# A fifth tile for du times B in a selective-scan network, taken from the pool behind the scan inputs

## The chip, the cores and the metric

The kernel runs on one core of a Trainium2 chip as one launch. The metric is the time of an execution on the device in microseconds; three runs of the kernel before have a median of 8846.92 us (8845.23 to 8850.76). One further execution was profiled. All data is float32.

## The reference

Four images of 64x64 tokens with 128 channels pass through four layers. Layer 0 is a block around a selective scan in four directions, then an MLP; layer 1 is a self-attention over all 4096 tokens; layer 2 is a chain of convolutions of 1x1 and 3x3; layer 3 is a neighbourhood attention with a 7x7 window, then an MLP. What matters here is the scan: `xs` are the activations of 256 channels in four orders (by rows, by columns, and both backwards), and every channel has 16 states.

```
def step(h, t):
    x_t, d_t, B_t, C_t = t
    h = jnp.exp(d_t[..., None] * A) * h + (d_t * x_t)[..., None] * B_t[:, :, None, :]
    return (h, jnp.einsum('bkdn,bkn->bkd', h, C_t))
...
h0 = jnp.zeros((Bn, K, DI, N), input.dtype)
_, ys_l = jax.lax.scan(step, h0, scan_in)
```

## The kernel before, in words

`scan_inputs` computes, for an image, delta, du = delta times x, B and C, and writes them to HBM. `selective_scan` reads them back in chunks of `LC` = 512 steps. For each image there are 4 directions, 8 chunks, 2 halves of the channels, 4 groups of states (`j`) and 2 pairs (`pp`): 512 rounds an image, 2048 in all. A round, called a unit in what follows, does this:

- GpSimd makes `dB` = du times B as one 128x1024 product (L500 and L501), into one of 4 tiles that are used in turn.
- ScalarE makes dA = exp(A times delta) in two halves of 128x512, in PSUM, where there are 3 tiles for it (L506, L507).
- VectorE runs two scans of 512 steps, which read dA and dB (L509).
- The product of the states with C goes to VectorE as two 128x512 operations (L514) or, in some units (`ON_POOL`: 5 of 16 in the first image, 7 of 16 later), to GpSimd as one 128x1024 operation (L522). Its tile is `hc`, from the class `Products`. A product on GpSimd is given out 2 units late (`BEHIND`).
- TensorE sums over the states with a matrix of ones and zeros (L555), and ScalarE copies the last state for the next chunk (L516, L518).

SyncE issues the loads of delta and du (4 tiles each) and of the rows of B and C (4 tiles each, L494).

Beside the scan of image 1, 2 or 3 the program holds `rest` of the image before it: the output of layer 0 with its MLP (`scan_output`), layers 1 and 2, and the attention of layer 3; the MLP of layer 3 is given out together with the `scan_output` of the next image. The `rest` of the last image follows its scan.

No order is written out by hand. A scheduler in the compiler puts the instructions of each engine in one fixed order, by priorities and by its own timing of the instructions, and adds the waits. The scan counts its priorities from `SCAN_FIRST` = 10,000,000. Each engine then runs its queue in order, and an instruction whose tile is still being read by others waits at the head of it.

Tile pools are taken from the core's memory like a stack. When the inputs of all images are made, their pools are given back; the pool `ss_more` is then opened in that place and stays open until the scans are over. `S.products.widen(more, 4)` lets the hc tiles use it: after 40 further tiles, 4 of 10 come from there. The pools of `rest` lie behind it.

The lines that the change and the prediction touch are L435, L438 to L451 (`Products`), L500 (the dB tile), L507, L509, L514, L522, and L1743 (`widen`). The edge memsets of layer 2, L985 and L987, are the only other instructions on GpSimd that repeat in each image while scans run.

Of the kernel before, what the change touches and what calls it, by code (L numbers as in the profile page):

```python
# [28 lines left out]
F32 = mybir.dt.float32  # L29
# [13 lines left out]
LC = 512  # L43
# [24 lines left out]
def mid(ap, n):  # L68

    return bc(ap.unsqueeze(1), [ap.shape[0], n, ap.shape[1]])  # L70
# [29 lines left out]
class Together:  # L100
# [3 lines left out]
    def __init__(self, tc, K):  # L104
        self.tc, self.K, self.done = tc, K, None
# [57 lines left out]
def loader(tc, pool, A, layer):  # L163
    def load(name, shape, src=None):
        t = pool.tile(shape, F32, name=f"w{layer}_{name}")
        tc.nc.sync.dma_start(t, A[f"L{layer}_conv_{name}"] if src is None else src)
        return t

    return load
# [240 lines left out]
def make_scan(ctx, tc, K, A):  # L410

    nc = tc.nc
    S = SimpleNamespace()
    big = ctx.enter_context(tc.tile_pool(name="ss_big", bufs=1))
    S.pool = ctx.enter_context(tc.tile_pool(name="ss", bufs=2))
    S.psum = ctx.enter_context(tc.tile_pool(name="ss_ps", bufs=1, space=PSUM))
    load = loader(tc, big, A, 0)
    S.A = load("A_log", [128, KD, NJS, NPR, 2])
    nc.scalar.activation(S.A, S.A, AF.Exp)
    nc.vector.tensor_scalar_mul(S.A, S.A, -1.0)  # L420
    ds4 = load("Ds", [128, ND, KD])
    total = big.tile([128, ND], F32, name="Dsum")
    nc.vector.tensor_reduce(total, ds4, AX.X, ALU.add)
    S.skip = big.tile([128, ND, 128], F32, name="skip_diag")
    for d in range(ND):
        nc.scalar.activation(S.skip[:, d, :], K.ident, AF.Copy, scale=total[:, d : d + 1])

    S.pick = big.tile([128, 32], F32, name="pick")
    nc.gpsimd.memset(S.pick, 1.0)
    for base, sign in ((0, 1), (3, -1)):  # L430
        nc.gpsimd.affine_select(
            S.pick, S.pick, [[-4 * sign, 32]], ALU.is_ge, 0.0, base=base, channel_multiplier=sign
        )
    S.unit = 0
    S.products = Products(S.pool)  # L435
    return S


class Products:

    def __init__(self, pool):
        self.pool, self.more, self.turn = pool, None, 0

    def widen(self, pool, bufs):
        self.more, self.bufs, self.turn = pool, bufs, -40

    def tile(self):
        self.turn += 1
        if self.more is not None and self.turn > 0 and self.turn % (6 + self.bufs) < self.bufs:
            return self.more.tile([128, 2, LC], F32, name="hc", bufs=self.bufs)  # L450
        return self.pool.tile([128, 2, LC], F32, name="hc", bufs=6)  # L451


def selective_scan(tc, K, S, D, img):
# [9 lines left out]
    pool, psum, products = S.pool, S.psum, S.products  # L464
    waiting = []

    def settle(unit):
        while waiting and waiting[0][0] <= unit:
            waiting.pop(0)[1]()

    for k in ORDER:
# [4 lines left out]
        for i in range(NCH):  # L476
            c = NCH - 1 - i if back else i
            for hf in range(2):
# [11 lines left out]
                for j in range(NJS):  # L490
# [6 lines left out]
                    hcs, made = [], []  # L497
                    for pp in range(2):
                        pr = 2 * hf + pp
                        dB = pool.tile([128, 2, LC], F32, name="dB", bufs=4)  # L500
                        nc.gpsimd.tensor_mul(dB, dus[pp], mid(bt, 2))  # L501
                        on_pool = S.unit % 16 in ON_POOL[img > 0]
                        S.unit += 1
                        hc = products.tile()
                        for g in range(2):
                            dA = psum.tile([128, LC], F32, name="dA", bufs=3)  # L506
                            nc.scalar.activation(dA, dts[pp][:, g, :], AF.Exp, scale=S.A[:, k, j, pr, g : g + 1])  # L507
                            hg = hc[:, g, :] if on_pool else dA
                            nc.vector.tensor_tensor_scan(  # L509
                                hg[:, order], dA[:, order], dB[:, g, order],  # L510
                                0.0 if i == 0 else state[:, j, pr, g : g + 1], ALU.mult, ALU.add,
                            )
                            if not on_pool:
                                mm = nc.vector.tensor_mul(hc[:, g, :], dA, ct)  # L514
                                if i < NCH - 1:
                                    nc.scalar.copy(state[:, j, pr, g : g + 1], dA[:, last : last + 1])  # L516
                        if on_pool and i < NCH - 1:
                            nc.scalar.copy(state[:, j, pr, :], hc[:, :, last])  # L518
                        if on_pool:

                            def product(hc=hc, ct=ct, made=made):
                                made.append(nc.gpsimd.tensor_mul(hc, hc, mid(ct, 2)))  # L522

                            waiting.append((S.unit + BEHIND, product))
                        else:
                            made.append(mm)
                        hcs.append(hc)
                        settle(S.unit)
# [1169 lines left out]
def network(tc, A, out):  # L1698
    nc = tc.nc
    with ExitStack() as ctx:  # L1700
        nc.scalar.preload_act_table_set("natural_log_exp_and_others")
        K = make_consts(ctx, tc)
        dram = ctx.enter_context(tc.tile_pool(name="scratch", bufs=1, space=DRAM))

        def scratch(name, shape):
            return dram.tile(shape, F32, name=f"{name}_dram")

        D = SimpleNamespace()
        D.bias = scratch("bias", [len(BIAS_KINDS), 128, HEADS * 512])
        D.biasT = [[scratch(f"biasT{k}_{i}", [128, HEADS, LC]) for i in range(4)] for k in range(3)]  # L1710
        D.conv_diag = scratch("conv_diag", [128, ND, 9, 128])
        D.w2_norms = scratch("w2_norms", [128, len(NORMS2), 4])
        D.w2_cv4, D.w2_bias = scratch("w2_cv4", [128, 128]), scratch("w2_bias", [1, 128])
        for name, shape in (("sz", [128, ND, LC]), ("xc", [128, ND, LC]), ("y", [128, ND, LC])):
            setattr(D, name, [[scratch(f"{name}{b}_{c}", shape) for c in range(NCH)] for b in range(B)])
        for name, shape in (("delta", [128, ND, LC]), ("du", [128, ND, LC]), ("bc", [NS, 2, LC])):
            made = [
                [[scratch(f"{name}{b}_{k}_{c}", shape) for c in range(NCH)] for k in range(KD)] for b in range(B)
            ]
            setattr(D, name, made)  # L1720
        D.y_first = [[[scratch(f"y_first{b}_{k}_{c}", [128, ND, LC]) for c in range(NCH)] for k in range(2)] for b in range(B)]
        D.y_cols = [scratch(f"y_cols{b}", [NCH, 128, NCH, ND, RC * RC]) for b in range(B)]
        for name in ("x4", "x5"):
            setattr(D, name, [scratch(f"{name}_{b}", [NT, C]) for b in range(B)])
        D.shift = [scratch(f"shift{b}", [NJ, 128]) for b in range(B)]

        with ExitStack() as scan_ctx:
            S = make_scan(scan_ctx, tc, K, A)
            make_conv_diagonals(tc, K, A, D.conv_diag)
            with priority(tc, K, SCAN_FIRST // 2):  # L1730
                with tc.tile_pool(name="mk_w2", bufs=1, side="right") as pool:
                    make_layer2(tc, K, A, D, pool)
            scan_inputs(tc, K, A, D, 0)
            before = None
            for img in range(B):
                with priority(tc, K, SCAN_FIRST):
                    selective_scan(tc, K, S, D, img)
                if img == 0:
                    make_bias(tc, K, A, D.biasT)
                    for later in range(1, B):  # L1740
                        scan_inputs(tc, K, A, D, later)
                    more = scan_ctx.enter_context(tc.tile_pool(name="ss_more", bufs=1))
                    S.products.widen(more, 4)  # L1743
                else:
                    rest(tc, K, A, D, img - 1, before)
                    before = img - 1, out[img - 1]
            rest(tc, K, A, D, B - 1, before, scan_ctx.close, out[B - 1])
        needed = ctx.enter_context(tc.tile_pool(name="needed", bufs=1)).tile([1, 1], mybir.dt.int32, name="needed")
        bound_exceeded(tc, K, needed)
        with tc.If(nc.values_load(needed) > 0):  # L1750
            everything_again(tc, K, A, D, out)
# [80 lines left out]
```

## Time and profile before

| | |
|---|---|
| median of three runs | 8846.92 us (8845.23 to 8850.76) |
| profiled execution | 8838.78 us, its span 8837.0 us |
| mean granted clock of TensorE | 0.860 |
| busy in the span: PE, DVE, ACT, POOL | 7047.0, 7137.4, 5686.9, 7046.7 us |
| dB products on GpSimd | 2048, mean 2375 ns |
| hc products on GpSimd | 832, mean 2376 ns |
| scans on VectorE | 4096 (four groups of L509, mean 1207 to 1272 ns) |
| last dB product ends | 7630 us after the start |

PE is TensorE's matmuls, DVE is VectorE, ACT is ScalarE, POOL is GpSimd and SP is SyncE. A row of a group gives the line, the engine, the operation, what it writes and reads with shapes, the count, then the busy time in us, the mean of one in ns, and the idle time of the engine just before these instructions with what ended most of it. A row of the waits gives the waiting engine with tile and line, what released it, and then the total in us, the number of times and the longest. "issue" stands where the profile shows no releaser. The stages of the program overlap, so shares over the whole span say little of one stage.

### The profile page before, as it was taken

The numbers are of one execution on the slowest core, as the hardware profiler recorded it, in microseconds if no ns is written. First come the engines' busy times: TensorE is split into PE (matmuls) and PEld (weight loads), VectorE is DVE, ScalarE is ACT, GpSimd is POOL, SyncE is SP. The second block draws the span as 40 slices with busy tenths as digits, with TensorE's granted clock in tenths as the row PEclk, the third lists the DMA queues.
The fourth block names the chain that finished last, engine by engine and source line by source line (L and its number), as shares of the span: only waits on it lengthen the run. The fifth ranks groups of instructions, "written<-read, shape, count | busy, mean of one in ns | idle before, by whom it ended". The sixth has DMA issues, their size and how long they took to land. (4 is left out here: it accounts for less than half of the span.)

```text
span 8837.0 us, 102218 instructions
## 1 busy us (share of the span) xinstructions
PE 7047.0 (80%) x30532; PEld 2635.0 (30%) x30532; DVE 7137.4 (81%) x8531; ACT 5686.9 (64%) x11661; POOL 7046.7 (80%) x3079
## 2 busy tenths in 40 slices
PE   6745858687788898786788988877789887788988
PEld 2211313132332222333322223333322223344333
DVE  4788978787999999998899999998899999513433
ACT  5646767676676676666766676667766666454366
POOL 6888998989899999997799999998899989500000
PEclk8756869697799998898899998888899998899989
DMA  5777777777554556665455556575455565320020
GB/s 185 244 232 247 241 251 240 260 242 262 189 170 165 170 170 219 191 211 190 160 168 173 174 174 227 194 224 176 156 171 174 176 217 192 108 70 5 1 82 12
DMA packets 855474, 1572.03 MB, mean 178 GB/s; under 512 B 218341, under 2 KB 336764, under 8 KB 851197
## 3 DMA queue, kind: packets, MB, share of 16 engines
q1 hardware_dynamic: 724605, 1389.21, 48.1%
q10 hardware_dynamic: 130304, 176.19, 5.6%
q8 instruction: 245, 4.01, 0.2%
q14 instruction: 320, 2.62, 0.1%
HBM read 1273.92 MB, written 280.18 MB: 176 GB/s over the span
## 5 line engine op out<-in xcount | busy, mean ns | idle before, releaser
L501 POOL TENSOR_TENSOR dB<-du,b_rows 128x1024 f32<-128x1024 f32 x2048 | 4805.9, 2375 | 477.2 <-issue 124.7
L507 ACT ACTIVATE dA<-dt,w_A_log 128x512 f32<-128x512 f32 x4096 | 2781.9, 690 | 510.8 <-DVE hc L509 246.7
L509 DVE TENSOR_TENSOR_SCAN dA<-dA,state,dB 128x512 f32<-128x512 f32 x2128 | 2631.5, 1272 | 275.6 <-POOL dB L501 131.8
L522 POOL TENSOR_TENSOR hc<-hc,c_rows 128x1024 f32<-128x1024 f32 x832 | 1976.6, 2376 | 47.0 <-ACT state L518 21.7
L509 DVE TENSOR_TENSOR_SCAN hc<-dA,state,dB 128x512 f32<-128x512 f32 x1456 | 1801.1, 1267 | 180.5 <-ACT dA L507 105.8
L514 DVE TENSOR_TENSOR hc<-dA,c_rows 128x512 f32<-128x512 f32 x2432 | 1564.5, 675 | 74.4 <-PE py L555 59.3
L555 PE MATMUL py<-hc,pick 128*32 128x512 f32 x8192 | 1245.1, 683 | 392.0 <-POOL hc L522 299.8
L516 ACT COPY state<-dA 128x1 f32<-128x1 f32 x2128 | 326.9, 158 | 1271.7 <-DVE hc L514 1260.1
L845 PE MATMUL pa<-e,l_v 128*128 128x512 f32 x2048 | 1062.5, 651 | 20.3 <-ACT e L801 20.3
L797 PE MATMUL pair<-l_g,l_f 32*128 32x512 f32 x2048 | 532.8, 667 | 165.7 <-ACT e L801 119.1
L801 ACT ACTIVATE e<-pair 128x1024 f32<-128x1024 f32 (+1 forms) x448 | 508.4, 1135 | 231.4 <-PE pair L797 222.8
L985 POOL MEMSET l_h<- 64x128 f32 x8 | 1.6, 197 | 814.9 <-DVE l_h L959 814.9
L845 PEld LDWEIGHTS pa<-e,l_v 128*128 128x128 f32 x2048 | 374.3, 199 | 670.9 <-issue 615.1
L555 PEld LDWEIGHTS py<-hc,pick 128*32 128x32 f32 x8192 | 210.1, 116 | 1161.4 <-issue 471.1
L247 PE MATMUL ps<-band,w_conv_diag 128*128 128x504 f32 (+3 forms) x1152 | 500.4, 594 | 6.0 <-ACT delta L397 6.0
L1351 PE MATMUL pair<-table,ident 128*128 128x512 f32 x768 | 408.2, 657 | 98.7 <-ACT e L1361 76.2
L509 DVE TENSOR_TENSOR_SCAN dA<-dA,dB 128x512 f32<-128x512 f32 x304 | 356.1, 1212 | 66.3 <-POOL dB L501 52.5
L201 PE MATMUL ps<-ident,ln_xn 128*128 128x128 f32 x512 | 141.9, 371 | 325.2 <-ACT ln_xn L198 253.2
L328 POOL TENSOR_TENSOR du<-delta,xc 128x1024 f32<-128x1024 f32 x128 | 333.3, 2611 | 52.6 <-ACT delta L397 46.7
L1361 ACT ACTIVATE e<-pair 128x1024 f32<-128x1024 f32 (+1 forms) x224 | 254.8, 1137 | 178.6 <-PE pair L1355 177.8
L247 PEld LDWEIGHTS ps<-band,w_conv_diag 128*128 128x128 f32 x1152 | 221.3, 193 | 283.9 <-issue 263.8
L797 PEld LDWEIGHTS pair<-l_g,l_f 32*128 32x128 f32 x2048 | 140.6, 189 | 523.9 <-ACT e L801 264.4
(285 smaller groups left out, 8746.8 us busy)
## 6 DMA issues: line engine op xcount, KB each, us to landing
b_rows<-bc_dram SPq DMA_DIRECT2D x1024, 256.0 KB
c_rows<-bc_dram SPq DMA_DIRECT2D x1024, 256.0 KB
dt<-delta_dram SPq DMA_DIRECT2D x512, 512.0 KB
du<-du_dram SPq DMA_DIRECT2D x512, 512.0 KB
delta_dram<-delta ACTq DMA_DIRECT2D x128, 512.0 KB
du_dram<-du SPq DMA_DIRECT2D x128, 512.0 KB
table<-biasT_dram SPq DMA_DIRECT2D x72, 512.0 KB
y_first_dram<-y_sum ACTq DMA_DIRECT2D x128, 256.0 KB
```

The costliest lines, as they stand in the source:

```text
L247: mm = nc.tensor.matmul(out[:, r0 - row0 : r1 - row0, c0:c1], lhsT((dy + 1) * 3 + dx + 1), src[:, r0 + dy : r1 + dy, c0 + dx : c1 + dx], s ...
L328: nc.gpsimd.tensor_mul(du.rearrange("p d (a b) -> p d a b", b=H), deltas[b].rearrange("p d (a b) -> p d a b", b=H), tk,)
L501: nc.gpsimd.tensor_mul(dB, dus[pp], mid(bt, 2))
L507: nc.scalar.activation(dA, dts[pp][:, g, :], AF.Exp, scale=S.A[:, k, j, pr, g : g + 1])
L509: nc.vector.tensor_tensor_scan(hg[:, order], dA[:, order], dB[:, g, order], 0.0 if i == 0 else state[:, j, pr, g : g + 1], ALU.mult, ALU.add,)
L514: mm = nc.vector.tensor_mul(hc[:, g, :], dA, ct)
L522: made.append(nc.gpsimd.tensor_mul(hc, hc, mid(ct, 2)))
L555: mm = nc.tensor.matmul(py[0][32 * q : 32 * q + 32, :], S.pick, hcs[q // 2][:, q % 2, :], start=(k == 1 and j == 0), stop=(j == NJS - 1),)
L797: nc.tensor.matmul(ps[:, u, :], f[quad, t // 4, span(t % 4, 128)], g[quad, c, :], start=True, stop=True)
L801: made = nc.scalar.activation(e, ps, AF.Exp)
L845: nc.tensor.matmul(pa, v[:, 8 * q + t, :], es[q], start=(t == 0 and q == 0), stop=(t == 7 and q == 3),)
L1351: nc.tensor.matmul(ps[:, u, :], K.ident, t[:, u, :], start=True, stop=False)
```

## The change

The class `Products` becomes `Tiles`, which takes the name of the tile and the number in the first pool, so that it serves the dB tiles too. dB tiles come from it, 4 from the scan's own pool. When `ss_more` has been opened, `S.inputs.widen(more, 1)` gives it one more tile there: after 40 further tiles, every fifth dB tile comes from `ss_more`. The pool grows by 4 KB in each partition, and the pools of `rest` behind it begin 4 KB higher. The instructions are the same in number and kind.

```diff
     S.unit = 0
-    S.products = Products(S.pool)
+    S.products = Tiles(S.pool, "hc", 6)
+    S.inputs = Tiles(S.pool, "dB", 4)
     return S
-class Products:
-    def __init__(self, pool):
-        self.pool, self.more, self.turn = pool, None, 0
-    def widen(self, pool, bufs):
-        self.more, self.bufs, self.turn = pool, bufs, -40
+class Tiles:
+    def __init__(self, pool, name, bufs):
+        self.pool, self.name, self.bufs = pool, name, bufs
+        self.more, self.turn = None, 0
+    def widen(self, pool, extra):
+        self.more, self.extra, self.turn = pool, extra, -40
     def tile(self):
         self.turn += 1
-        if self.more is not None and self.turn > 0 and self.turn % (6 + self.bufs) < self.bufs:
-            return self.more.tile([128, 2, LC], F32, name="hc", bufs=self.bufs)
-        return self.pool.tile([128, 2, LC], F32, name="hc", bufs=6)
+        pool, bufs = self.pool, self.bufs
+        if self.more is not None and self.turn > 0 and self.turn % (self.bufs + self.extra) < self.extra:
+            pool, bufs = self.more, self.extra
+        return pool.tile([128, 2, LC], F32, name=self.name, bufs=bufs)
...
-                        dB = pool.tile([128, 2, LC], F32, name="dB", bufs=4)
+                        dB = S.inputs.tile()
                         nc.gpsimd.tensor_mul(dB, dus[pp], mid(bt, 2))
...
                     S.products.widen(more, 4)
+                    S.inputs.widen(more, 1)
```

## The prediction

> **What bounds the kernel now.** I read four views in this order: the page's busy times and groups, the busy times by stage, the waits of GpSimd (POOL) in one stage, and the timeline there. The page's chain that ended last covers only the final microseconds (it starts at about 8800 us) and says nothing on the scan. From the page, GpSimd and its two groups:
>
> ```profile
> PE 7047.0 (80%) x30532; PEld 2635.0 (30%) x30532; DVE 7137.4 (81%) x8531; ACT 5686.9 (64%) x11661; POOL 7046.7 (80%) x3079
> ...
> L501 POOL TENSOR_TENSOR dB<-du,b_rows 128x1024 f32<-128x1024 f32 x2048 | 4805.9, 2375 | 477.2 <-issue 124.7
> ...
> L522 POOL TENSOR_TENSOR hc<-hc,c_rows 128x1024 f32<-128x1024 f32 x832 | 1976.6, 2376 | 47.0 <-ACT state L518 21.7
> ```
>
> These two groups are nearly all of GpSimd's 7046.7 us, and the last dB ends at 7630 us: until there GpSimd is over 90% busy. One dB tile with its two scans (a "unit") costs it in images 1 to 3 2.375 + 7/16 x 2.376 = 3.41 us. Where its idle time lies is seen by stage; the columns are the stretch, its length, then busy time (and count) of PE, PEld, DVE, ACT and POOL, PE's clock, DMA share and GB/s:
>
> ```profile
> 2215.00:2580.00 365.00, 284.03 (x1264) 142.23 (x1260) 331.20 (x429) 240.82 (x542) 309.51 (x134) 0.83 0.56 180
> 2580.00:3250.00 670.00, 601.81 (x2444) 177.53 (x2442) 634.45 (x689) 453.11 (x861) 670.00 (x291) 0.92 0.52 172
> 3250.00:3400.00 150.00, 129.49 (x564) 39.99 (x561) 140.96 (x181) 104.96 (x227) 118.99 (x55) 0.87 0.55 174
> 3400.00:3980.00 580.00, 470.62 (x2678) 178.61 (x2677) 546.22 (x608) 375.48 (x772) 580.00 (x251) 0.88 0.65 209
> 3980.00:4445.00 465.00, 337.95 (x1364) 167.90 (x1364) 379.31 (x537) 324.23 (x735) 367.15 (x159) 0.82 0.54 174
> 4445.00:5150.00 705.00, 636.40 (x2618) 193.57 (x2610) 666.59 (x715) 474.14 (x904) 700.25 (x303) 0.94 0.53 172
> 5150.00:5310.00 160.00, 134.71 (x601) 41.20 (x602) 154.97 (x199) 115.98 (x244) 136.47 (x64) 0.86 0.56 183
> 5310.00:5900.00 590.00, 481.78 (x2708) 181.65 (x2706) 557.41 (x622) 381.03 (x792) 590.00 (x255) 0.88 0.65 210
> 5900.00:6375.00 475.00, 363.13 (x1474) 181.97 (x1474) 409.06 (x560) 342.00 (x751) 390.99 (x170) 0.83 0.54 175
> 6375.00:7050.00 675.00, 607.96 (x2482) 181.97 (x2482) 636.43 (x685) 453.74 (x879) 675.00 (x292) 0.94 0.53 175
> ```
>
> The stages alternate. In the long ones (attention of layers 1 and 3) GpSimd is busy all the time and is the bound. In six stages it is not: three long ones with the layer-0 output and MLP of the image before (idle 365 - 309.5 = 55.5, 97.9 and 84.0 us) and three short ones with its layer 2 (31.0, 23.5 and, by the row of 7050 to 7215 us, 25.6 us): 317 us together. In the short ones VectorE (DVE) is 94 to 98% busy; in the long ones it idles 33.8, 85.7 and 65.9 us itself. In the worst stage, 3985 to 4440 us, GpSimd's waits begin so:
>
> ```profile
> POOL dB L501 <- issue: 29.7, 9, 8.4
> POOL dB L501 <- DVE hc L509: 17.0, 9, 4.6
> ```
>
> "issue" hides the same cause, as the timeline there shows (start, length, engine):
>
> ```profile
> 4231.01 1.28 DVE L509 TENSOR_TENSOR_SCAN dA<-dA,state,dB 128x512 f32<-128x512 f32 x1
> ...
> 4232.43 2.37 POOL L501 TENSOR_TENSOR dB<-du,b_rows 128x1024 f32<-128x1024 f32 x1 [2.94 <-issue]
> ...
> 4234.98 2.44 DVE L509 TENSOR_TENSOR_SCAN hc<-dA,state,dB 128x512 f32<-128x512 f32 x2
> ...
> 4237.57 2.37 POOL L501 TENSOR_TENSOR dB<-du,b_rows 128x1024 f32<-128x1024 f32 x1 [2.77 <-DVE hc L509]
> ```
>
> Both dB products start 0.14 to 0.15 us after a scan ends. I set every dB of images 1 to 3 beside the scans that read the tile which held its buffer before: GpSimd stands 278.5 us before dB products in all, and 269.2 us of it (137 gaps) ends at the last of those scans. So the ring of four dB tiles is full, and these are the waits that the change touches. Between the first and the last such gap of a stage no scan waits for a dB: VectorE, not GpSimd, sets the pace while the ring is full.
>
> **What the Trainium skill says.** "Perfetto Trace Analysis", section "Optimization Strategy", reads the same gap repeated on the engine that should be saturated as a possible lack of room for the next tile; the 137 gaps agree. The same section speaks of regimes whose most contended engine changes; the table agrees. "SBUF — State Buffer", section "Who interferes with whom", says that a VectorE operation with at most one SBUF input doesn't contend with GpSimd. The scans and products read dA from PSUM, and dB products took 2.33 to 2.54 us in the whole trace, so more overlap should cost nothing.
>
> **The change part by part.** It removes and adds no instruction: 2048 dB products, 4096 scans and all others have the same counts in both programs. The renamed class hands out the hc tiles as before. *Ring:* 299 of the 1536 dB tiles of images 1 to 3 lie in the new 4 KB, from the 42nd of image 1 on (2338 us now), so all six full stages except the start of the first have it. When VectorE falls behind, GpSimd can run one dB further before it stands: 2.36 us. Nothing empties the ring within a stage, so this is won once a stage, not once a gap: 6 x 2.36 = 14 us. GpSimd, busy before and after, carries it to the end of the scan. *Addresses:* pools opened later lie 4 KB higher; of the attention's tiles that share bytes with the next xT, two e buffers instead of one: nothing, as the attention ends before the next xT is opened either way. *The scan's end:* VectorE has the same 721 other instructions after its last scan in both orders, so the last 1200 us move along whole.
>
> *Order.* The scheduler, knowing of the fifth tile, orders all queues anew from image 1 on. The two memset lines of layer 2 are landmarks on GpSimd: the first stands behind 816, 1354 and 1890 dB products instead of 813, 1348 and 1886. So before layer 2, that is over each image's long full stage, the scans are 3, 6 and 4 units further against the layer work. If the chip's layer work keeps its pace, each unit takes 3.41 us out of GpSimd's idle time: 13 x 3.41 = 44 us, which includes the ring's share there, and is within the idle time of GpSimd (237 us) and VectorE (185 us). The lead is on the scheduler's clock, not the chip's, and no trace shows it; it could be worth nothing, or cost (rival 3). Bounds for a lead that helps: 14 us (ring alone) and 44 + 3 x 2.36 (the ring in the short stages) = 51 us. I take some 10 of the 37 us between, 24 us in all: nothing here shortens VectorE's waits for ScalarE, which are most of its idle time there. On SyncE's queue the row loads move by few places; of GpSimd's waits in the worst stage 4.7 us are put down to b_rows, so I cost that at nothing within the bounds.
>
> Sum: the profiled execution took 8838.8 us (span 8837.0); minus 24 is 8814.8. The median of the runs stands 8.1 us above it, so 8846.9 - 24 = 8823 us.
>
> **Rivals.** (1) The ring alone, order neutral: VectorE bounds the full stages, 14 us or less: 8833 us, within 0.2%. For: no scan there waits for a dB. Against: the new order. (2) The new order also suits VectorE: in the long full stages it waits for dA exponentials 17.8, 48.0 and 47.1 us, 113 us in all; if half of that goes too, 14 + 56 = 70 us, 8777 us. For: those scans head VectorE's queue while their exponential stands behind layer work on ScalarE. Against: the edit touches no wait of ScalarE. (3) Slower: ScalarE takes the place of the ring. ScalarE's queue is in order, and exponentials drawn ahead of layer work can stand at its head until a dA bank comes free, with the layer's activations behind them, for which TensorE and then VectorE wait. VectorE's waits there are GpSimd's. Half as much again as the 113 us is 56 us, less 14: 42 us slower, 8889 us. It decides over 0.2% from 14 + 18 = 32 us. (4) That the tile isn't used is excluded by the count of 299; its first use waits for the last image's scan inputs, whose convolutions end by 2046 us.
>
> **How the numbers follow.** 0.2% is 17.7 us, about what a measurement of this kernel can tell from none. Forecast (14 to 51 us, own range 8796 to 8833): 0.50; rival 1 (8833 to 8850): 0.28; rival 2: 0.08; rival 3: 0.14. Faster: 0.44 of the first (the rest gains under 17.7) and 0.08: 0.52. Slower: 0.13 of rival 3. Same: the rest, 0.35. Range: from 8795, where the forecast's own ends, to 8850, where rival 1 ends; rivals 2 and 3 lie outside, about 2 in 10.
>
> **What would show it.** Ring: GpSimd's idle time in the six stages falls from 317 by 14 to 51 us, the last dB ends near 7606 us, gaps still end at scans. Order: layer 2 begins at about the same time with 3 to 6 more dB done. Wrong: VectorE's waits for dA over 113 us in the long stages (rival 3), or idle time on GpSimd in the attention stages, where there is none now.

## The result and the profile after

The kernel after takes 8799.14 us (median of 6 runs, 8787.25 to 8805.84), the kernel before, timed beside it, 8846.08 us (6 runs, 8833.55 to 8850.76). The ratio is 0.9944, 95% interval [0.9934, 0.9953]: 47 us faster. The profiled execution took 8797.75 us with a span of 8795.8 us; before it was 8838.78 and 8837.0 us. The gain is real, lies inside the range given, and is twice the 24 us of the forecast. The experiments show that one of the two steps that made up those 24 us gives nothing by itself.

The lines of the page that answer to those of before (line numbers from the change on are 3 higher: the dB product is L504, the scan L512, the exponential L510, the hc product on GpSimd L525, its state copy L521):

```profile
PE 6999.8 (80%) x30532; PEld 2613.9 (30%) x30532; DVE 7141.1 (81%) x8531; ACT 5683.3 (65%) x11661; POOL 7049.4 (80%) x3079
...
L504 POOL TENSOR_TENSOR dB<-du,b_rows 128x1024 f32<-128x1024 f32 x2048 | 4835.5, 2406 | 416.0 <-DVE hc L512 112.3
...
L525 POOL TENSOR_TENSOR hc<-hc,c_rows 128x1024 f32<-128x1024 f32 x832 | 2003.9, 2409 | 64.4 <-ACT state L521 29.1
```

Counts and busy times stand as they were (VectorE 7137.4 to 7141.1 us, GpSimd 7046.7 to 7049.4). What changed is idle time: in front of dB products 477.2 to 416.0 us, in front of hc products on GpSimd 47.0 to 64.4 us. The first fell by 61, the second rose by 17, and the difference of 44 us is about the gain of 41 us between the two spans.

The busy times by stage of the kernel after, with the six stretches in which the ring of dB tiles fills first and two attention stretches behind them (columns as before: the stretch, its length, then busy time and count of PE, PEld, DVE, ACT and POOL, PE's clock, DMA share, GB/s):

```profile
2220.00:2570.00 350.00, 261.60 (x1184) 136.40 (x1176) 315.87 (x413) 229.53 (x519) 295.12 (x127) 0.84 0.55 176
3275.00:3425.00 150.00, 121.18 (x532) 38.93 (x528) 138.80 (x178) 105.24 (x226) 125.46 (x57) 0.87 0.58 193
4000.00:4440.00 440.00, 331.88 (x1351) 166.05 (x1348) 381.58 (x533) 321.78 (x734) 364.84 (x158) 0.82 0.57 182
5180.00:5305.00 125.00, 101.56 (x458) 31.79 (x454) 123.36 (x161) 86.27 (x177) 108.55 (x49) 0.88 0.59 183
5895.00:6365.00 470.00, 348.26 (x1468) 169.38 (x1468) 411.06 (x564) 342.94 (x755) 394.78 (x171) 0.85 0.56 182
7060.00:7180.00 120.00, 104.44 (x490) 33.30 (x486) 119.59 (x159) 86.50 (x164) 104.45 (x47) 0.92 0.55 172
2570.00:3275.00 705.00, 632.25 (x2601) 188.72 (x2602) 672.45 (x728) 477.82 (x914) 704.86 (x307) 0.94 0.53 175
4440.00:5180.00 740.00, 668.16 (x2757) 200.51 (x2758) 703.41 (x758) 502.73 (x961) 737.59 (x321) 0.93 0.52 172
```

GpSimd idles 350 - 295.12 = 54.9, 24.5, 75.2, 16.5, 75.2 and 15.6 us in the six, 262 us in all where it was 317; the stages of attention still leave it no gap (0.1 and 2.4 us). The long stage of image 1 gained nothing (55.5 to 54.9); the largest gain is in that of image 2 (97.9 to 75.2). There, from 4000 to 4440 us, GpSimd's waits begin so:

```profile
POOL dB L504 <- DVE hc L512: 20.5, 13, 4.4
POOL dB L504 <- issue: 10.5, 6, 2.7
POOL hc L525 <- ACT state L521: 8.9, 8, 2.2
```

So a ring of five fills as well. Set beside the scans that read each buffer's earlier tile, 213.1 of the 216.8 us of gaps in front of dB products in images 1 to 3 end at such a scan (before 269.2 of 278.5). The waits of VectorE from 2180 to 7580 us, first before, then after (columns: waiting engine, tile and line, releaser, total us, times, longest):

```profile
DVE hc L509 <- ACT dA L507: 91.6, 53, 7.0
DVE dA L509 <- POOL dB L501: 80.7, 90, 5.1
DVE dA L509 <- ACT dA L507: 59.1, 38, 4.6
DVE hc L509 <- POOL dB L501: 41.5, 51, 2.8
```

```profile
DVE hc L512 <- ACT dA L510: 89.3, 63, 4.9
DVE dA L512 <- POOL dB L504: 85.5, 104, 5.1
DVE dA L512 <- ACT dA L510: 43.9, 31, 4.9
...
DVE hc L512 <- POOL dB L504: 11.9, 11, 2.3
```

Its scans wait 151 and then 133 us for exponentials (143 in a second profile of the kernel after), and 122 and then 97 us for dB products. Its waits in this stretch add up to 408 us before and 366 us after, and no single one carries the difference.

Where in time the gain comes from, I read at the first edge memset of layer 2 in each image, by counting the dB products that have ended. Image 1: 812 at 3241.5 us before, 815 at 3255.9 us after. Image 2: 1347 at 5159.3 us, 1354 at 5155.1 us. Image 3: 1885 at 7061.0 us, 1889 at 7042.0 us. At 3.41 us a unit the scan after is 4 us behind at the first, 7 x 3.41 + 4.2 = 28 us ahead at the second, 33 us at the third and 40 us at its end (7630.4 to 7590.8 us). The 4 us lost at the first landmark lie ahead of image 1: its first dB product starts at 2161.7 us before and at 2166.7 us after, though up to there the order is the same.

### The profile page after: what moved, and what is told of

Same layout as the page of the kernel before. It is cut to its first block, busy times and chain, and to the rows that moved or that the text cites. A ratio compares the mean times of both kernels' runs of the same rounds, so it can differ in the third digit from the quotient of the medians.

```text
span 8795.8 us, 102113 instructions
## 1 busy us (share of the span) xinstructions
PE 6999.8 (80%) x30532; PEld 2613.9 (30%) x30532; DVE 7141.1 (81%) x8531; ACT 5683.3 (65%) x11661; POOL 7049.4 (80%) x3079
## 5 line engine op out<-in xcount | busy, mean ns | idle before, releaser
L504 POOL TENSOR_TENSOR dB<-du,b_rows 128x1024 f32<-128x1024 f32 x2048 | 4835.5, 2406 | 416.0 <-DVE hc L512 112.3
L510 ACT ACTIVATE dA<-dt,w_A_log 128x512 f32<-128x512 f32 x4096 | 2781.3, 690 | 481.7 <-DVE hc L512 217.8
L512 DVE TENSOR_TENSOR_SCAN dA<-dA,state,dB 128x512 f32<-128x512 f32 x2128 | 2629.6, 1272 | 273.8 <-POOL dB L504 134.9
L525 POOL TENSOR_TENSOR hc<-hc,c_rows 128x1024 f32<-128x1024 f32 x832 | 2003.9, 2409 | 64.4 <-ACT state L521 29.1
L512 DVE TENSOR_TENSOR_SCAN hc<-dA,state,dB 128x512 f32<-128x512 f32 x1456 | 1804.3, 1267 | 148.2 <-ACT dA L510 110.5
L512 DVE TENSOR_TENSOR_SCAN dA<-dA,dB 128x512 f32<-128x512 f32 x304 | 355.9, 1211 | 62.2 <-POOL dB L504 51.7
```

The source lines that it names most:

```text
L512: nc.vector.tensor_tensor_scan(hg[:, order], dA[:, order], dB[:, g, order], 0.0 if i == 0 else state[:, j, pr, g : g + 1], ALU.mult, ALU.add,)
```

## The experiments

Two theories were at odds. By the first the tile itself gives the gain, since GpSimd can run one product further. By the second the gain is the scheduler's: with another pool it places all instructions anew, and the new order suits the chip better, whether the tile is there or not. Later came a third question: is the new order a lucky draw, or are orders made for five tiles better as a rule?

**Repetition.** The kernel after, once more, beside the next three runs, with no edit.

> The changed kernel as it stands, timed beside the three others: about 8799 us, 47 us under the kernel before.

Measured: 8795.5 us against 8850.9 us, ratio 0.9943 [0.9929, 0.9957]. In images 1 to 3 the gaps before dB products are 218.1 us (216.8 in the first profile) and VectorE's idle time is 371.0 us (377.7): such figures repeat within some 7 us.

**Five tiles in the order of before.** The program is built once with four tiles, each engine's order is read off, and the build with five tiles must keep it on all queues (SyncE's among them). In the traces VectorE, ScalarE, GpSimd and SyncE's transfers run in the order of before, instruction by instruction.

```diff
-                    S.inputs.widen(more, 1)
+                    if tc.ring == 5:
+                        S.inputs.widen(more, 1)
...
+    nc = build(5, order_of(build(4)))
```

> Five dB tiles, but every queue in exactly the order of the kernel before (the scheduler is run once with four tiles, and its order is imposed on the program with five). Theory A (the ring is worth one dB product a full stage, the rest of the gain is the new order): 14 us under the kernel before, 8832 us, and in each of the six full stages GpSimd's idle time falls by about 2.4 us. Rival B (the ring alone does it all): about 8799 us.

Measured: 8857.56 us, ratio 1.0011 [1.0002, 1.0019]. In this order the tile gives nothing. (Four tiles under an imposed order were not timed; a cost of imposing it is not excluded, but the busy times of VectorE, ScalarE and GpSimd are within 5 us of those before.) Both expectations, 8832 and 8799 us, are missed. Yet the tile does its own job: the groups of GpSimd in this run's page are

```profile
L504 POOL TENSOR_TENSOR dB<-du,b_rows 128x1024 f32<-128x1024 f32 x2048 | 4797.1, 2368 | 285.4 <-DVE dA L512 78.5
...
L525 POOL TENSOR_TENSOR hc<-hc,c_rows 128x1024 f32<-128x1024 f32 x832 | 1969.2, 2367 | 243.6 <-ACT state L521 195.4
```

The idle time in front of dB products falls by 192 us, from 477.2 to 285.4, many times the 14 us that I gave the ring. The hc products take it all: their idle time rises by 197 us, from 47.0 to 243.6. The timeline of this run in the long stage of image 2, for ScalarE, GpSimd and the scans, shows how:

```profile
4235.45 4.65 POOL L504 TENSOR_TENSOR dB<-du,b_rows 128x1024 f32<-128x1024 f32 x2
...
4237.31 2.45 DVE L512 TENSOR_TENSOR_SCAN hc<-dA,state,dB 128x512 f32<-128x512 f32 x2
...
4237.82 1.28 ACT L226 ACT_TABLE_LOAD   x1
...
4239.12 2.42 ACT L226 ACTIVATE mlp_h<-ps,w_fc_b 128x512 f32<-128x512 f32 x4
...
4241.56 1.28 ACT L96 ACT_TABLE_LOAD   x1
...
4242.86 1.30 ACT L510 ACTIVATE dA<-dt,w_A_log 128x512 f32<-128x512 f32 x2
...
4243.63 2.47 DVE L512 TENSOR_TENSOR_SCAN dA<-dA,state,dB 128x512 f32<-128x512 f32 x2 [3.87 <-issue]
...
4244.10 0.18 ACT L521 COPY state<-hc 128x2 f32<-128x2 f32 x1
...
4244.35 2.36 POOL L525 TENSOR_TENSOR hc<-hc,c_rows 128x1024 f32<-128x1024 f32 x1 [4.25 <-ACT state L521]
```

GpSimd makes two dB products without a stop, then the hc product is at the head of its queue and stands 4.25 us until the state copy on ScalarE is done. The scans that the copy reads ended at 4239.76 us, but on ScalarE it is queued behind 1.28 + 2.42 + 1.28 = 4.98 us of the MLP of the image before, with a table load (ScalarE's change to another set of functions) on either side, and behind two exponentials. A scan of VectorE idles 3.87 us in the same hole, whose end is the first exponential after it. The room for one more dB product lets GpSimd reach the hc product sooner, and that one can't be done sooner. The Trainium skill, "Perfetto Trace Analysis", section "Per-engine timelines", calls the queues of ScalarE, VectorE and GpSimd strictly first in, first out; this row agrees, since the next dB product stood behind the hc product although the scans that read its buffer in the ring of five had ended at 4239.76 us too. The table load is 1283 ns long in this run; "ScalarE: Activation LUTs", section "What ACT_TABLE_LOAD costs", gives the same figure, and some 1380 ns for a drain with every change of set. The drain does not show here: from the start of a load to the start of ScalarE's next instruction the median is 1295 ns.

**The same with GpSimd's queue left to the scheduler.** One could say that the forced order of GpSimd spoils the tile. So this one keeps the order of before on the four other engines only.

```diff
     for engine, names in order.items():
+        if "Pool" in engine:
+            continue
```

> Five dB tiles; VectorE, ScalarE, TensorE and SyncE in exactly the order of the kernel before, GpSimd's own order left to the scheduler (in the run old_order_ring5 it was the old one too). Theory D (with the old order a dB that no longer stands for its buffer only lets the hc product behind it stand for its state, and what VectorE does is unchanged): the same as the kernel before within 0.2%, 8851 us. If the old order of GpSimd's own queue was what held the ring back (theory E): about the gain that new_order_ring4 lacks, 30 us, 8820 us.

Measured: 8871.23 us against 8846.87 us, ratio 1.0030 [1.0019, 1.0042]: still no gain. VectorE's waits of this run from 2180 to 7580 us:

```profile
DVE hc L512 <- ACT dA L510: 210.8, 195, 7.0
DVE dA L512 <- ACT dA L510: 74.6, 61, 4.6
...
DVE dA L512 <- POOL dB L504: 12.6, 9, 5.1
```

Scans wait almost no more for dB products (122 us before, 18 us with a row of 5.3 us that is not shown). They wait 285 us for exponentials, where it was 151. The wait of the ring was traded for one for ScalarE, as rival 3 has it, at a price of 24 us.

Two things in the traces say more. First, GpSimd's own order. In images 1 to 3 an hc product stands in its queue behind 3.9 dB products of later units (the mean) before, in the order just held, and in every four-tile kernel below; with five tiles and an order of its own GpSimd has 4.9, here as in the kernel after. So the 237 us in front of hc in the run before this one come of holding an order made for four tiles: here it is 57 us. Theory E is out, and theory D, which kept that wait and the time, is right in neither. Second, the place. VectorE has the same order in this run and before, so the stages can be compared from unit to unit, with the edges of the prediction's table. The six full stages take 3 us more than before, those of attention 31 us more. In attention the scans waited 108 us for dB before and 3.5 here, and 35 and 161 us for exponentials. The room does reach these stages, but ScalarE is late there as soon as GpSimd is not.

**The order of after with four tiles.** VectorE, ScalarE, TensorE and SyncE keep the order of after; GpSimd's order is free; that its order for five tiles can't run with four was assumed, not tried. The edit is that of the run before with the two builds exchanged:

```diff
+    nc = build(4, order_of(build(5)))
```

> Four dB tiles, but VectorE, ScalarE, TensorE and SyncE in exactly the order of the changed kernel; only GpSimd's own order is left to the scheduler, since its order with five tiles can't run with four. Theory A: most of the gain is here, 8846 - (47 - 14) = 8813 us. Rival B: no gain, 8846 us or more. Rival C (order and ring need each other: scans drawn ahead find no dB without the fifth tile): slower than the kernel before, with scans on VectorE waiting for dB in the full stages.

Measured: 8831.55 us, ratio 0.9976 [0.9968, 0.9983], 19 us faster than before; the kernel after, timed beside it, was 55 us faster. So the order without the tile gives a third to a half of the gain, which lies between theories A (8813 us) and B (no gain), and C is out. Its waits of VectorE in the same stretch:

```profile
DVE hc L512 <- ACT dA L510: 154.2, 136, 5.6
DVE dA L512 <- ACT dA L510: 53.8, 42, 4.9
DVE dA L512 <- POOL dB L504: 46.5, 53, 5.1
DVE hc L512 <- POOL dB L504: 25.4, 29, 2.3
```

The profiled execution of this run is one of its slower ones: 8838.21 us, where its 16 lie between 8811.75 and 8842.88. It is no faster than the profiled one of before (8838.78 us), so what follows from the two profiles shows where waits went, not the 19 us.

The four kernels make a square, in ratios to the kernel before. Order of before: 1 with four tiles, 1.0011 with five. Order of after: 0.9976 with four, 0.9943 with five. The tile costs about 10 us in the order made without it and gives 8851 x 0.0033 = 29 us in the order made with it. One limit stands: GpSimd's own order is the same in the first two corners and not in the last two. With GpSimd's order left to the scheduler in all four, the corner of five tiles in the order of before is the run above with 1.0030: then the tile costs some 27 us in the one order and gives 29 us in the other.

The same square in the trace, for the stretch from the first dB product of image 1 to the last of image 3 (us, worked out from each profile; the first repetition of after beside it):

| | length | GpSimd idle before dB | before hc | VectorE idle |
|---|---|---|---|---|
| before | 5468.7 | 278.5 | 41.1 | 427.0 |
| five tiles, order of before | 5482.9 | 80.5 | 237.5 | 436.4 |
| the same, GpSimd free | 5497.9 | 291.2 | 57.3 | 456.0 |
| order of after, four tiles | 5458.5 | 262.2 | 45.7 | 416.3 |
| after | 5424.0 | 216.8 | 58.3 | 377.7 |
| after, repeated | 5419.5 | 218.1 | 54.9 | 371.0 |

The gaps in front of dB products, on which the prediction was built, don't follow the length: 80.5 us goes with a slow run, 216.8 with the fastest. VectorE's idle time follows it to 7 us, because the work of VectorE in the stretch is the same everywhere (5041.7 to 5048.5 us, length less idle time).

Part of the order's effect can be placed. ScalarE has 40 batches of MLP activations between two table loads in this stretch; with 0.6 us behind each they fill some 230 us, 4% of it, and hold 104 of VectorE's 418 idle us before (counted from 2180 to 7600 us). With the order of after it is 87 us, with four tiles as with five; with that of before and five tiles 105 us. Outside the batches VectorE idles 313 us before, 324 with the order of after and four tiles, and 288 with both. So the order takes 17 us out of the batches, but adds 11 us to the rest as long as there are four tiles; the tile, once the order is made for it, takes 36 us out of the rest. From unit to unit, most of what the tile gives there lies in the stages of attention: 22 to 32 of 33 us, by where the edges are set. Scans wait there 98 to 108 us for exponentials with four tiles and 34 to 41 with five, while those for dB products rise from 50 to 80. Why exponentials come sooner with the fifth tile was not looked into.

**A sixth tile, taken from the hc ring.** In the same pool, two further dB tiles and three further hc tiles.

```diff
-                    S.products.widen(more, 4)
-                    S.inputs.widen(more, 1)
+                    S.products.widen(more, 3)
+                    S.inputs.widen(more, 2)
```

> Six dB tiles, and nine hc tiles instead of ten from image 1 on, in the same memory as the changed kernel; ordered by the scheduler. Theory A: the ring adds another 14 us to the gain, and the new order can go either way by 20 us: 8785 us within 20. If hc tiles are short with nine, GpSimd and VectorE wait for TensorE's sums and the time rises above 8799 us.

Measured: 8913.79 us, ratio 1.0073 [1.0059, 1.0086], 63 us slower than before and 118 us slower than after. The expectation, 8785 us within 20, is missed by far. Two things were changed here, and the scheduler's order is a third. VectorE's waits of this run from 2180 to 7650 us show a row that is new:

```profile
DVE dA L512 <- ACT dA L510: 97.0, 61, 4.9
DVE hc L512 <- ACT dA L510: 90.4, 62, 4.9
DVE hc L517 <- DMA c_rows<-bc_dram: 74.7, 44, 5.9
```

The products of VectorE stand 75 us for the rows of C, where it was 2 us before and 19 us after. The sign that the expectation names for too few hc tiles shows as well: what VectorE writes into hc tiles waits 26 us for TensorE's sums, where it was 1 us before and after. The rows have four tiles, and their next load can start only when the last product with the old ones is done. That fits a scan which runs further ahead of its rows, but which of the three changes makes the kernel slower was not separated.

**Other draws of the order.** Here the tiles are used from another product on, which by itself moves few products to another buffer but makes the scheduler place everything anew. First, after with the fifth tile used 80 products after the widening in place of 40, and the kernel before, still with four dB tiles, with its further hc tiles used after 80:

```diff
-                    S.inputs.widen(more, 1)
+                    S.inputs.widen(more, 1, -80)
```

```diff
-                    S.products.widen(more, 4)
+                    S.products.widen(more, 4, -80)
```

> The changed kernel, with the fifth tile used after 80 further tiles instead of 40, which gives the scheduler another draw of its order with the same ring. If five tiles bring about a better order as a rule: 8800 us within 10. If the order of the changed kernel is one draw among many: anything between 8780 and 8860 us.

> The kernel before with four dB tiles, with the further hc tiles used after 80 tiles instead of 40: another draw of the order with the old ring. If four tiles hold the order back as a rule: 8850 us within 10. If orders are draws: as far from 8850 as the changed kernel is, to either side.

Measured: 8787.47 us, ratio 0.9936 [0.9919, 0.9952], and 8795.85 us, ratio 0.9941 [0.9924, 0.9957]. The first, with five tiles, lies a little below the 8800 us within 10 that a rule would give. The second is the surprise of the study: with four tiles and nothing but another draw of the order, the kernel gains 51 us, as much as the change. In its profile (8806.74 us, its slowest execution) the stretch of images 1 to 3 is 18 us shorter than before and what follows it 20 us shorter (1187.0 us in place of 1206.5). So the 47 us alone don't show that the fifth tile is worth anything.

To tell a lucky draw from a rule, I made pairs with four and five dB tiles, whose further hc tiles start after 60, 30 and 80 products. The edit is the second of the two above with -60, -30 or -80, with and without the line for the fifth tile.

> Four dB tiles as in the kernel before; only the count of products after which the four further hc tiles come into use is 60 in place of 40, which makes the scheduler place the work anew. Theory A (the orders that the scheduler gives are draws that scatter by some 50 us, and the fifth tile is worth at most 14 us beside them): anywhere between 8790 and 8860 us; VectorE idle in the scan images' window follows the time. Theory B (five tiles are worth the 47 us as a rule, and the one fast four-tile order was a lucky one): 8835 to 8860 us, near the kernel before.

> The partner of the kernel with 60, with five dB tiles (the fifth after 40 products, as in the change). Theory A: its difference to that four-tile partner lies anywhere between -50 and +30 us. Theory B: 30 to 60 us below the partner, near 8800 us.

> Four dB tiles, the further hc tiles after 30 products in place of 40: one more order with the ring of before. Theory A: between 8790 and 8860 us. Theory B: 8835 to 8860 us.

> The partner of the kernel with 30, with five dB tiles. Theory A: difference to its four-tile partner anywhere between -50 and +30 us, and the mean over all pairs within 25 us of nothing. Theory B: 30 to 60 us below the partner, near 8800 us.

> The partner of the fast four-tile order (further hc tiles after 80 products, 8795.85 us), with five dB tiles. The three pairs so far (40, 60, 30) gave five less four tiles -47, -19 and -59 us. Theory A (the differences are the scatter of orders round a worth of at most 14 us): between -40 and +40 us, 8755 to 8835 us, as likely above the partner as below it. Theory B (an order made for five tiles is better by some 40 us as a rule, whichever start is taken): 8740 to 8775 us. Between them (the order of 80 has already what five tiles would give): within 15 us of the partner.

| hc tiles start after | four dB tiles | five dB tiles | five less four |
|---|---|---|---|
| 40 (before, after) | 8846.08 us, 1 | 8799.14 us, 0.9944 [0.9934, 0.9953] | -47 us |
| 60 | 8836.25 us, 0.9989 [0.9981, 0.9998] | 8816.94 us, 0.9963 [0.9950, 0.9975] | -19 us |
| 30 | 8834.50 us, 0.9987 [0.9980, 0.9994] | 8775.59 us, 0.9921 [0.9905, 0.9938] | -59 us |
| 80 | 8795.85 us, 0.9941 [0.9924, 0.9957] | 8796.17 us, 0.9941 [0.9924, 0.9958] | 0 us |

Neither theory holds as it was put. The differences average (47 + 19 + 59 - 0) / 4 = 31 us in favour of five tiles; they scatter with a standard deviation of 27 us, so the mean of four pairs has a 95% interval of some 43 us to either side and doesn't exclude nothing. The kernel whose fifth tile starts at 80 (8787.47 us) has the kernel before as its partner and would add a fifth difference, -59 us, that is not independent of the first. Of these expectations, theory A had the mean within 25 us of nothing, theory B every pair at 30 to 60 us; the pairs with 60 and 80 are against B, the mean leans against A. Four-tile orders of the scheduler lie between 8796 and 8846 us, its five-tile orders between 8776 and 8817 us.

The lowest time, 8775.59 us, is that of the pair with 30: 23 us below the kernel after. Its VectorE waits from 2180 to 7580 us for the exponentials are the shortest but one of all these runs:

```profile
DVE dA L512 <- POOL dB L504: 100.9, 118, 5.1
DVE hc L512 <- ACT dA L510: 87.9, 75, 4.5
DVE dA L512 <- ACT dA L510: 36.2, 24, 5.3
```

124 us for exponentials against 133 and 143 after and 151 before. These waits don't rank the kernels, though: the fast four-tile kernel with 80 has 165 us. The pair's kernel also owes 24 us to the end: from its last dB product to the end of the span 1182.2 us pass, 1206.5 before and 1205.0 after. In the five-tile kernel with 80 these are 1165.2 us, and its stretch of images 1 to 3 is 11 us longer than its partner's (5461.3 to 5450.2). So the order also decides how much layer work is left for the end, where TensorE is the busiest engine (83 to 93% of each 300 us from 7800 to 8700 us in the kernel after). I did not try to shift that by itself.

## Why the prediction was right, and where it was wrong

**The outcome.** The sign and the range were right: 8799 us lies in 8795 to 8850, near its lower end. The forecast of 8823 us was 24 us too high, and only a part of its reasons stands. That the total fell into the range is partly luck: the order is one draw of several, and two of the five-tile draws, 8787 and 8776 us, lie below the range.

**Ring: 6 x 2.36 = 14 us, carried by GpSimd to the end of the scan.** This step failed. With the order of before held, five tiles gave +0.1% in place of -0.16%, and with GpSimd's order free +0.3%. The working asked what the dB product waits for and stopped there. With GpSimd's order held, the wait moved by one instruction: 192 us gone in front of dB, 197 back in front of the hc product, which waits for a scan and a copy that hang on ScalarE. With GpSimd's order free, the room was carried, and the kernel was slower all the same: in the stages of attention, where the working had GpSimd as the bound, the scans' waits for dB fell by 105 us and those for exponentials rose by 127. The size does not hold either: with the order held 192 us of waits for the ring went, not 14 us at six places. (By the code the first tile in the new room is the 45th of image 1, at 2352 us, not the 42nd; nothing hangs on it.)

**Order: 14 to 51 us with the ring, 24 taken.** The bounds held (41 us between the profiled executions, 47 between the medians), and the choice inside them was too low by half. The measure was doubtful, though. At the landmarks 3, 7 and 4 more dB products were done, close to the 3, 6 and 4 read from the order. But the 3 of image 1 came with a layer 2 that began 14 us later and were worth nothing, while at the one of image 2, which began 4 us sooner, the scan was 28 us ahead. The four-tile order with 80 has no more products ahead than before (its first memsets stand behind 807, 1348 and 1882 dB products, against 813, 1348 and 1886) and gains 51 us. A lead in the list is no lead on the chip, as the prediction feared, and it doesn't rank orders.

**The two steps were added, and they don't add.** The sum took the ring and the order as two terms. By its ratios the square of four kernels gives +10 us for the tile alone (+27 with GpSimd's order free), -21 us for the order alone and -50 us for both: 39 us (56) come only with both. Nothing in the prediction had a place for that.

**"Nothing here shortens VectorE's waits for ScalarE."** Wrong, if not by much. In the three long stages VectorE's waits for exponentials were 17.8, 47.2 and 47.1 us by the rows before (112 us), and 22.1, 26.6 and 40.6 us after (89 us; 90 in the repetition). The 23 us sit nearly all in image 2, where the largest gain is. Rival 2 had the place right and, with 56 us, the size too large by more than two.

**The scan's end moves along whole.** Right for this change: 1206.5 to 1205.0 us from the last dB product to the end of the span. Not a law: other orders made it 1165 to 1241 us. (Behind the last scan the traces have 581 instructions of VectorE, not 721, but as many in both.)

**Addresses: nothing.** In accord with the runs, as the kernel that has the new addresses and the order of before gained nothing; by themselves they were not tried.

**What would show it.** GpSimd's idle time in the six stages fell by 55 us (14 to 51 said; by the whole stretch 324.0 to 279.4 us, 45 us), the last dB product ended at 7591 us (7606 said), gaps still end at scans, waits for exponentials stayed under 113 us in the long stages, and the two stages of attention shown have next to no gaps. The first two went further than said; all the signs point the way that was said, and they would have let the ring's step pass as confirmed. Only the runs that held an order told the tile from the order.

**Rivals.** Rival 1, the ring alone at 8833 us, had the ring alone gain 14 us; alone it takes 8858 us. Rival 3 is what happens when the order of VectorE and ScalarE is held: ScalarE takes the ring's place, at +10 to +27 us in place of +42. Rival 4 is out: dB waits change in every run with five tiles.

**What stays open.** Which feature of an order makes it fast is known in part (17 us in ScalarE's batches). Why the fifth tile shortens the waits for exponentials in the order of after, and lengthens them in that of before, is not known. Whether five tiles are better over many orders, by the 31 us of four pairs, or whether these pairs were kind, would need more pairs.

## What to carry to other kernels

A buffer that removes a wait gains only if nothing else is late at the same place. Before you price it, follow the producer's queue one instruction further (here to hc), and ask what else the reader needs (here the exponentials). Where a scheduler orders the program, any edit is also a new draw of its order; build a few neighbours that differ in nothing that should matter, measure their scatter (here 8796 to 8846 us), and believe a gain of that size only when the change wins in pairs, or with the order held. Then use the scatter: the best kernel here is a draw, too.

## What the runs showed that was not expected

- A change that touches where a few tiles lie, and no instruction, moved the time by 51 us (0.6%) through the order alone.
- Deepening the ring of dB from four to five with the order held changed where GpSimd waits by some 195 us and the time by 0.1%.
- A batch of ScalarE with another table takes 4.98 us for 2.42 us of work (two table loads of 1.28 us each), and the 40 batches beside the scans hold a quarter of VectorE's idle time in 4% of the time.
- The mean of the dB row rose from 2375 to 2406 ns after, and to 2433 ns in the four-tile order with 80, without more busy time of GpSimd (7046.7, 7049.4 and 7049.4 us) and in faster kernels. The records of neighbouring products then overlap more; what sets that was not looked into.
